# A transformer's first layer: the order of owed work, fillers, taps and divisors

## The chip, the cores and the metric

The kernel runs on one core of one Trainium2 chip. The metric is the device time of one execution in microseconds (us); a time is the median of several executions. PE is the matmul engine (TensorE; PEld are its weight loads), DVE is VectorE, ACT is ScalarE, POOL is GpSimd, and SP issues the DMAs.

## The reference, cut to what matters

Two gated layers run over x (8 sequences of 224 tokens, 512 wide). Each layer is a cross attention on a context of 750 tokens, and a feed-forward part. The change touches the first layer only: 16 heads of 32, and a feed-forward part with ternary weights and a depthwise convolution of three taps.

```
x = x + tanh(g_xattn[0]) * xattn0(layernorm(x), ctx)      # 16 heads, softmax over 750 keys
x = x + tanh(g_ffn[0])   * ffn0(layernorm(x))
    # ffn0: bit_linear 512 -> 2048, conv over 3 tokens, silu, bit_linear 2048 -> 512
x = x + tanh(g_xattn[1]) * xattn1(layernorm(x), ctx, mask) # 8 heads
x = x + tanh(g_ffn[1])   * ffn1(layernorm(x))              # fp4 weights and activations
```

## The kernel before

The program is written out in full, batch after batch: batches n = 0 to 7 are the first layer's attention (`attention16`), n = 8 to 15 the second layer's (`attention8`), and the second layer's feed-forward part closes the kernel. Every engine runs its instructions in the order in which the program issues them.

**A batch of attention16** has two halves. In the first, 16 slots (4 groups of heads, 2 halves of the queries, 2 halves of the context) form the scores of four heads in two pairs of PSUM banks (`ps_pair`, L485); VectorE takes their negated maxima (L493), and ScalarE the exponentials for the sums (L502). Both `ps_pair` tiles are in use by one slot, so the next slot's scores wait for its exponentials. Then the maxima of both context halves are joined (`val`, L526), split into three bf16 parts (`stat_rows`, L427 and L431), and transposed on PE (L437, copied by ScalarE at L439). In the second half, 12 steps form the scores again, transposed and with the maxima taken off (L449, L458), ScalarE takes the exponentials (L601), and PE multiplies them with the values (`products`, L576). What the sums are divided by is worked out in between, in five pieces of the generator `divisors` (named `more`): `less` on VectorE and its exponential on ScalarE (L539, L540); sums, reciprocal and bf16 parts on VectorE (L543 to L546, L427, L431); their transpose (L437, copied at L439); and two spreads over the partitions (L555, copied at L563). The products of two groups are divided at L584.

**Fillers.** Between these fixed parts the program puts pieces of other work, each from a generator that yields its declared cost on PE and on VectorE:

- `values` (L374, copied by ScalarE at L383): 24 pieces of 0.86; `project_out` of the batch before (L398, L409): 8 of 0.86; `ffn0_out` of the batch two before (L1021, L1031): 8 of 0.86.
- `keys_queries` of the next batch: keys (L312, copied by ScalarE at L321) in pieces of 0.63, and between them the norm of x (L172 to L182, `qxn` here), its transposes (L194, copied at L195) and the queries (L341, L350).
- `ffn0` of the batch before, mostly VectorE's: norm and quantization of x (L172 to L177, L182, L880, L859 to L865, L883, L885; one half of x is called fxq here), transposes (L194), spread scales (L210, L213), then eight groups of hidden columns: product (L907, into `ps_t`), scaled by VectorE (L915), the middle tap on ScalarE (L921, `middle`), the outer taps on VectorE (L935), tanh on ScalarE (L965), the gate on VectorE (L947), and a running maximum (L951, L959). Then the second quantization (L986, L989, L1007, L1010).

The tap on ScalarE is not issued at once: `product` puts it on a list (`deferred`), and `put_off` issues what is on it.

**The planner.** `owed` is PE work that was issued ahead of its due, `behind` is VectorE work that was issued and not yet worked off. `fill(us, queues)` takes pieces from the first queue that has any until `owed` reaches us, then takes us off. `pace(us, queues)` takes pieces while `behind` is under us. `finish(queue)` empties a queue and sets `owed` to 0. The queues are `soon` (the first four pieces of values, and project_out), `early` (ffn0_out and the other values), `late` (keys_queries), `beside` (this batch's ffn0) and `old` (what is left of the last one).

```
            self.fill(1.7, soon, early, late)
            if slot == 3:
                self.finish(soon)
                self.finish(old)
            ...
            more = min(max(self.behind - 2.3, 0), 0.5)
            self.fill(1.4 + more, soon, early, late)
            self.behind = max(self.behind - 2.3 - more, 0)
```

**PSUM tiles** on the way of this: `ps_m` (two) for keys, values, projections, queries and their transposes; `ps_t` (one) for the products of ffn0, all spreads and the small transposes; `ps_pair` (two); `ps_pa` (one) for the products with the values.

Of the kernel before, what the change touches and what calls it, by code (L numbers as in the profile page):

```python
# [63 lines left out]
class Net:  # L64
# [122 lines left out]
    def transposed(self, dst, src, i, bank="t"):  # L187

        nc = self.nc
        half = src.dtype == BF16  # L190
        pt = self.ps(bank, [128, KC, TP], BF16 if half else F32)
        ident = self.ident16 if half else self.ident
        for k in range(KC):
            nc.tensor.transpose(pt[:, k, :], src[:, k * 128 : (k + 1) * 128], ident[:TP, :TP])  # L194
        nc.scalar.copy(dst[:, :, i * TP : (i + 1) * TP], pt)  # L195
# [270 lines left out]
    def attention16(self, n, before, ahead, old, soon, early, late, beside):  # L466

        nc, pool, job = self.nc, self.att, self.jobs[n]
        kT, qT = job["kT"], job["qT"]
        rows = [slice(h * 32, (h + 1) * 32) for h in range(4)]


        part = pool.tile([TP, 2, NT, KC, 4], F32, name="part")
        sums = pool.tile([TP, 2, NT, KC, 4], F32, name="sums")
        slots = KC * NT * 2
        self.behind = 1.0  # L480
        for slot in range(slots):
            g, i, c = slot // (2 * NT), slot // 2 % NT, slot % 2
            sc = [self.ps("pair", [TP, 2, 512]) for _ in range(2)]
            for h, r in enumerate(rows):
                nc.tensor.matmul(  # L485
                    sc[h // 2][:, h % 2, :MH],
                    lhsT=qT[r, g, i * TP : (i + 1) * TP],
                    rhs=kT[g][r, c * MH : (c + 1) * MH],
                    start=True,
                    stop=True,  # L490
                )
            for k in range(2):
                nc.vector.tensor_reduce(  # L493
                    part[:, c, i, g, 2 * k : 2 * k + 2], sc[k][:, :, :MH], AX.X, ALU.max, negate=True
                )
            if slot == 0:
                self.finish([before])

                shown = pool.tile([CP, 4, 2 * S], F32, name="p", bufs=2)
            self.put_off()  # L500
            for h in range(4):
                nc.scalar.activation(  # L502
                    shown[:TP, h, :MH],
                    sc[h // 2][:, h % 2, :MH],
                    AF.Exp,
                    bias=part[:, c, i, g, h : h + 1],
                    accum_out=sums[:, c, i, g, h : h + 1],
                )


            self.fill(1.7, soon, early, late)
            if slot == 3:
                self.finish(soon)
                self.finish(old)
            elif slot < 3:
                self.pace(1.0, old)
            if slot in (10, 11):

                self.behind += next(ahead)[1]
            if (slot > 2 or n == 0) and slot < slots - 1:  # L520
                self.pace(1.0, beside)
            more = min(max(self.behind - 2.3, 0), 0.5)
            self.fill(1.4 + more, soon, early, late)
            self.behind = max(self.behind - 2.3 - more, 0)
        val = pool.tile([TP, NT, KC, 4], F32, name="val")
        nc.vector.tensor_tensor(val, part[:, 0], part[:, 1], ALU.min)  # L526
        transposed = self.stat_rows(self.stat[0][n % 2], val.rearrange("p t g h -> p t h g"))
        self.pace(1.0, beside)
        self.fill(1.3, early, late)
        self.finish(early)  # L530
        sT = transposed()
        self.fill(0.7, late)
        self.behind = max(self.behind - 2.5, 0)

        def divisors():

            less = pool.tile([TP, 2, NT, KC, 4], F32, name="less")
            for c in range(2):
                nc.vector.tensor_tensor(less[:, c], val, part[:, c], ALU.subtract)  # L539
            nc.scalar.activation(less, less, AF.Exp)  # L540
            self.behind += 0.4
            yield
            nc.vector.tensor_tensor(sums, sums, less, ALU.mult)  # L543
            total = pool.tile([TP, NT, KC, 4], F32, name="total0")
            nc.vector.tensor_tensor(total, sums[:, 0], sums[:, 1], ALU.add)
            nc.vector.reciprocal(total, total)  # L546
            transposed = self.stat_rows(self.stat_inv, total.rearrange("p t g h -> p t h g"))
            self.behind += 2.2
            yield
            iT = transposed()  # L550
            yield
            for pair in range(2):
                pi = self.ps("t", [128, 2, S])
                for k in range(2):
                    nc.tensor.matmul(  # L555
                        pi[:, k, :],
                        lhsT=self.spread_q[:, 2 * pair + k, :],
                        rhs=iT,
                        start=True,
                        stop=True,  # L560
                    )
                across[pair] = pool.tile([128, 2, S], F32, name="inv")
                nc.scalar.copy(across[pair], pi)  # L563
                yield

        aT = job["aT"] = pool.tile([128, KC, S], F32, name="aT")
        more, across, banks = divisors(), {}, {}

        def products(g, j0, p):

            if g % 2 == 0 and j0 == 0:
                banks["pa"] = self.ps("pa", [128, 2, S])
            for j in (j0, j0 + 1):
                for h, r in enumerate(rows):
                    col = g * 128 + h * 32
                    nc.tensor.matmul(  # L576
                        banks["pa"][r, g % 2, :],
                        lhsT=job["v"][j][:, col : col + 32],
                        rhs=p[:, h, (j - j0) * S : (j - j0 + 1) * S],
                        start=j == 0,  # L580
                        stop=j == NKT - 1,
                    )
            if g % 2 and j0 + 2 == NKT:
                nc.vector.tensor_tensor(  # L584
                    aT[:, g - 1 : g + 1, :], banks["pa"], across[g // 2], ALU.mult
                )
                self.behind += 0.6

        last = None
        for step in range(KC * NKT // 2):  # L590
            g, j0 = divmod(2 * step, NKT)
            pw = [self.ps("pair", [CP, 2, 512]) for _ in range(2)]
            k = kT[g][:, j0 * CP : (j0 + 2) * CP]
            self.weights_minus_max(
                [(pw[h // 2][:, h % 2, : 2 * S], r, g, qT[:, g, :], k) for h, r in enumerate(rows)],
                self.pick, sT, True,
            )
            p = pool.tile([CP, 4, 2 * S], F32, name="p", bufs=2)
            self.put_off()
            for k in range(2):  # L600
                nc.scalar.activation(p[:, 2 * k : 2 * k + 2, :], pw[k][:, :, : 2 * S], AF.Exp)  # L601
            self.behind = max(self.behind - 3.2, 0)
            if last:
                products(*last)
            last = g, j0, p
            if step in (0, 1, 3, 4, 8):
                next(more)
            self.fill(0.5, late)

            self.pace(1.0 if step in (5, 6) else 2.5, beside)  # L610
            self.fill(0.7, late)
        self.finish(late)

        def rest():
            products(*last)
            yield 0.8, 0.6

        return rest()
# [938 lines left out]
```

## Time and profile before

| | us |
|---|---|
| median of 3 runs (2151.72 to 2155.82) | 2153.29 |
| the profiled execution | 2156.02 |
| its span, first to last instruction | 2154.2 |
| PE busy in the span | 2107.8 |
| VectorE busy | 1362.9 |
| ScalarE busy | 1002.1 |
| mean granted PE clock | 0.998 |

The span begins with the first instruction of the program. A row of a timeline has the start, the time from first to last of the merged instructions, engine, line, operation, what is written and read, the count, and in brackets the engine's idle time before it with what ended it. One fp32 matmul stands as two MATMUL rows. A row of windows has the stretch, its length, the busy time and count of PE, PEld, DVE, ACT and POOL, the granted PE clock, the DMA share and GB/s. A row of waits has who waited for whom, the sum in us, the number of times, and the longest.

### The profile page before, as it was taken

The page shows a single profiled execution, that of the slowest core. Times are in us where ns is not written, and L with a number is a line of the kernel's source. Part 1 is how long each engine was busy: PE and PEld are TensorE (multiplying, and loading weights), DVE is VectorE, ACT ScalarE, POOL GpSimd, SP SyncE. Part 2 cuts the span into 40 slices and gives each one's busy share as a digit, 9 for nine tenths or more (in the row PEclk, how much of TensorE's full clock was granted, in tenths as well). Part 3 has the DMA queues.
Part 4 walks back from the last instruction along what each step waited for, and adds up shares of the span by engine and source line. Part 5 has one row for each costly group of instructions (what it writes and reads, how often), then busy time and mean ns, then how long its engine had stood idle before and what let it go on. Part 6 is the DMA issues. An engine that isn't in the chain of part 4 may idle for free.

```text
span 2154.2 us, 32130 instructions
## 1 busy us (share of the span) xinstructions
PE 2107.8 (98%) x12606; PEld 1213.0 (56%) x12606; DVE 1362.9 (63%) x2795; ACT 1002.1 (47%) x2332; POOL 130.3 (6%) x146
## 2 busy tenths in 40 slices
PE   9999999999999999999999999999999999999999
PEld 5444545455554545455656575666656565665555
DVE  3776666677767676674456575654723467776665
ACT  3566667575767667573444343443534331111111
POOL 0000000000000000000000010111100001111111
PEclk9999999999999999999999999999999999999999
DMA  7200010100001010111011112112110011000000
GB/s 226 78 31 29 2 46 2 32 15 18 29 2 46 2 46 21 52 35 52 15 32 52 52 44 66 42 56 69 57 46 11 14 52 41 10 20 20 20 6 20
DMA packets 50215, 81.24 MB, mean 38 GB/s; under 512 B 3344, under 2 KB 29712, under 8 KB 49936
## 3 DMA queue, kind: packets, MB, share of 16 engines
q1 hardware_dynamic: 50064, 79.18, 11.7%
q8 instruction: 100, 1.64, 0.3%
q14 instruction: 51, 0.42, 0.1%
HBM read 65.28 MB, written 13.89 MB: 37 GB/s over the span
## 4 chain that ended last, share of the span: by engine, by line
PE 88%; DVE 5%; ACT 4%; issue 1%; DMA 0%; SPq 0%; POOL 0%; ACTq 0%; POOLq 0%; DVEq 0%
PE ps_m L374 15%; PE ps_m L312 13%; PE ps_big L1168 11%; PE ps_m L1200 6%; PE ps_pair L485 6%; PE ps_m L398 5%; PE ps_m L341 4%; PE ps_half L703 4%; PE ps_half L763 4%; PE ps_pa L666 4%; PE ps_pair L458 2%; ACT p L601 2%; PE ps_pa L576 2%; PE ps_t L907 2%; PE ps_m L1168 2%; PE ps_t L1021 1%
## 5 line engine op out<-in xcount | busy, mean ns | idle before, releaser
L502 ACT ACTIVATE p<-ps_pair,part 112x375 f32<-112x375 f32 x512 | 286.3, 571 | 192.0 <-DVE part L493 192.0
L312 PE MATMUL ps_m<-cx,wk 128*128 128x375 f32 x1024 | 370.5, 491 | 1.3 <-ACT kT L321 1.1
L374 PE MATMUL ps_m<-wv,cx 128*125 128x512 f32 x768 | 355.4, 602 | 0.0
L493 DVE TENSOR_REDUCE part<-ps_pair 112x2 f32<-112x750 f32 x256 | 228.2, 932 | 130.4 <-PE ps_pair L485 128.5
L312 PEld LDWEIGHTS ps_m<-cx,wk 128*128 128x128 f32 x1024 | 179.7, 191 | 118.0 <-issue 34.4
L374 PEld LDWEIGHTS ps_m<-wv,cx 128*125 128x125 f32 x768 | 135.5, 187 | 159.7 <-issue 158.0
L720 DVE CUSTOM_DVE_ANT_0 ps_half<-ps_half,mbias 112x750 f32<-112x750 f32 x128 | 121.1, 946 | 150.7 <-PE ps_half L703 150.0
L601 ACT ACTIVATE p<-ps_pair 125x896 f32<-125x896 f32 x192 | 165.0, 911 | 76.9 <-PE ps_pair L458 76.9
L485 PE MATMUL ps_pair<-kT,qT 32*112 32x375 f32 x1024 | 148.0, 522 | 0.2
L741 ACT ACTIVATE p<-ps_half,nm 112x750 f32<-112x750 f32 x128 | 113.4, 890 | 66.0 <-DVE nm L732 65.6
L1200 PE MATMUL ps_m<-wd,hqT 128*128 128x512 f32 x308 | 136.6, 592 | 0.0
L383 ACT COPY v<-ps_m 125x512 f32<-125x512 f32 x96 | 56.5, 589 | 152.2 <-PE ps_m L374 151.5
L935 DVE SCALAR_TENSOR_TENSOR y<-hp,cw,y 128x224 f32<-128x224 f32 x256 | 109.4, 448 | 20.2 <-ACT y L921 15.7
L398 PE MATMUL ps_m<-wo,aT 128*112 128x512 f32 x256 | 119.6, 602 | 0.0
L1179 ACT ACTIVATE gth<-ps_big 128x352 f32<-128x352 f32 x48 | 22.2, 463 | 206.9 <-PE ps_big L1168 206.9
L341 PE MATMUL ps_m<-xnT,wq 128*128 128x224 f32 x512 | 113.2, 360 | 0.6 <-ACT xnT L195 0.6
L1168 PE MATMUL ps_big<-wu,xqT 128*128 128x352 f32 x352 | 111.3, 459 | 0.0
L1168 PE MATMUL ps_big<-wg,xqT 128*128 128x352 f32 x352 | 111.3, 459 | 0.0
L768 ACT COPY p<-ps_half 125x672 f32<-125x672 f32 x128 | 85.9, 722 | 49.9 <-PE ps_half L763 49.7
L485 PEld LDWEIGHTS ps_pair<-kT,qT 32*112 32x112 f32 x1024 | 52.1, 170 | 98.7 <-ACT p L502 69.6
L502 ACT ACTIVATION_READ_ACCUMULATOR p<-ps_pair,part 112x1 f32 x512 | 103.5, 202 | 0.0
L763 PEld LDWEIGHTS ps_half<-ident,p 112*125 112x125 f32 x768 | 93.2, 189 | 16.1 <-issue 7.8
(223 smaller groups left out, 3026.4 us busy)
## 6 DMA issues: line engine op xcount, KB each, us to landing
cx<-in_ctx SPq DMA_DIRECT2D x32, 750.0 KB, 4.4
wst<-in_w SPq DMA_DIRECT2D x16, 512.0 KB, 8.1
x<-in_x SPq DMA_DIRECT2D x8, 448.0 KB, 6.0
mid<-x SPq DMA_DIRECT2D x8, 448.0 KB, 3.1
x<-mid SPq DMA_DIRECT2D x8, 448.0 KB, 3.5
last<-x SPq DMA_DIRECT2D x8, 448.0 KB, 3.1
out<-yout SPq DMA_DIRECT2D x14, 256.0 KB, 2.0
wraw<-in_w_gate SPq DMA_DIRECT2D x11, 256.0 KB, 2.6
```

What stands on the lines that cost most here:

```text
L312: nc.tensor.matmul(pk, lhsT=self.w["wk"][:, k, g * 128 : (g + 1) * 128], rhs=job["cx"][c][:, k, :], start=k == 0, stop=k == KC - 1,)
L341: nc.tensor.matmul(pq[:, g - g0, :], lhsT=self.w["wq"][:, k, g * 128 : (g + 1) * 128], rhs=xnT[:, k, :], start=k == 0, stop=k == KC - 1,)
L374: nc.tensor.matmul(pv, lhsT=job["cx"][c][:, k, at : at + CP], rhs=self.w["wv"][:, k, :], start=k == 0, stop=k == KC - 1,)
L398: nc.tensor.matmul(po, lhsT=aT[:, g, i * TP : (i + 1) * TP], rhs=self.w["wo"][:, g, :], start=g == 0, stop=g == KC - 1,)
L485: nc.tensor.matmul(sc[h // 2][:, h % 2, :MH], lhsT=qT[r, g, i * TP : (i + 1) * TP], rhs=kT[g][r, c * MH : (c + 1) * MH], start=True, stop= ...
L493: nc.vector.tensor_reduce(part[:, c, i, g, 2 * k : 2 * k + 2], sc[k][:, :, :MH], AX.X, ALU.max, negate=True)
L502: nc.scalar.activation(shown[:TP, h, :MH], sc[h // 2][:, h % 2, :MH], AF.Exp, bias=part[:, c, i, g, h : h + 1], accum_out=sums[:, c, i, g, ...
L601: nc.scalar.activation(p[:, 2 * k : 2 * k + 2, :], pw[k][:, :, : 2 * S], AF.Exp)
L720: nc.vector.tensor_tensor_reduce(out=src, in0=src, in1=masks[i], scale=1.0, scalar=-MASKED, op0=ALU.add, op1=ALU.max, accum_out=mx,)
L763: nc.tensor.transpose(pt[:, j // half, j % half * TP : (j % half + 1) * TP], p[:, h, j * CP : (j + 1) * CP], self.ident[:TP, :TP],)
L1168: nc.tensor.matmul(ps[:, :CW], lhsT=xqT[:, k, :], rhs=wt[:, k, c0 : c0 + CW], start=k == 0, stop=k == KC - 1,)
L1200: nc.tensor.matmul(po, lhsT=hqT[:, k, :], rhs=wd[:, k, :], start=k == 0, stop=k == NC1 - 1)
```

## The change

In the slots: at slot 3, what is left of `soon` and `old` is issued ahead of the filler of 1.7 and not behind it. The second filler of each slot is 1.5 and not 1.4. At the join of the maxima, 1.7 is booked to `behind`, and the pace there goes to 2.7 and not to 1.0. In the steps: ScalarE's put-off taps go ahead of the exponentials only while `behind` is under 4.5, and behind them otherwise. The piece of `divisors` that belongs to a step is issued at the step's end and not ahead of its fillers. Steps 5 and 6 pace to 1.5 and not to 1.0, and a step's last filler is 0.6 and not 0.7. No instruction is added or left out.

```diff
-            self.fill(1.7, soon, early, late)
             if slot == 3:
                 self.finish(soon)
                 self.finish(old)
-            elif slot < 3:
+            self.fill(1.7, soon, early, late)
+            if slot < 3:
                 self.pace(1.0, old)
...
             more = min(max(self.behind - 2.3, 0), 0.5)
-            self.fill(1.4 + more, soon, early, late)
+            self.fill(1.5 + more, soon, early, late)
             self.behind = max(self.behind - 2.3 - more, 0)
...
-        self.pace(1.0, beside)
+        self.behind += 1.7
+        self.pace(2.7, beside)
         self.fill(1.3, early, late)
...
-            self.put_off()
+            late_vector = self.behind > 4.5
+            if self.behind < 4.5:
+
+                self.put_off()
             for k in range(2):
                 nc.scalar.activation(p[:, 2 * k : 2 * k + 2, :], pw[k][:, :, : 2 * S], AF.Exp)
+            self.put_off()
             self.behind = max(self.behind - 3.2, 0)
             if last:
                 products(*last)
             last = g, j0, p
+            self.fill(0.5, late)
+
+            self.pace(1.5 if step in (5, 6) else 2.5, beside)
+            self.fill(0.6, late)
             if step in (0, 1, 3, 4, 8):
+
                 next(more)
-            self.fill(0.5, late)
-
-            self.pace(1.0 if step in (5, 6) else 2.5, beside)
-            self.fill(0.7, late)
         self.finish(late)
```

## What the change will do to the time

> **What bounds the kernel now.** I read the page first, then PE's row of one batch of the first layer, then PE's waits, then single slots in the timeline. Page and windows:
>
> ```profile
> PE 2107.8 (98%) x12606; PEld 1213.0 (56%) x12606; DVE 1362.9 (63%) x2795; ACT 1002.1 (47%) x2332; POOL 130.3 (6%) x146
> ```
>
> ```profile
> 510.80:631.30 120.50, 117.60 (x858) 62.12 (x850) 83.95 (x163) 80.03 (x204) 1.38 (x2) 1.00 0.07 22
> ```
>
> PE sets the end; a batch (n=2 to 6) takes 120.5 us, 2.9 us of it idle by PE's row. The row hides most of the loss. Two consecutive slots of the timeline:
>
> ```profile
> 514.73 0.90 PE L485 MATMUL ps_pair<-kT,qT 32*112 32x375 f32 x8
> ...
> 515.56 2.83 PE L398 MATMUL ps_m<-wo,aT 128*112 128x512 f32 x6
> 515.67 1.79 DVE L493 TENSOR_REDUCE part<-ps_pair 112x2 f32<-112x750 f32 x2
> ...
> 516.70 0.57 ACT L502 ACTIVATE p<-ps_pair,part 112x375 f32<-112x375 f32 x1 [2.12 <-DVE part L493]
> ...
> 518.32 1.64 PE L485 MATMUL ps_pair<-kT,qT 32*112 32x375 f32 x8
> ...
> 519.08 0.27 PEld L485 LDWEIGHTS ps_pair<-kT,qT 32*112 32x112 f32 x4 [0.48 <-ACT p L502]
> ```
>
> Scores unhindered hold PE 0.83 (514.73 to 515.56). Their banks are free again when the fourth exponential is done: 519.08, 4.35 us after the slot began. Here PE had three filler matmuls (2.76 us) and stood in the second half of the next scores: 1.64 instead of 0.90, with no idle time in PE's row. So a slot costs nothing extra if its filler lasts 4.35 - 0.83 = 3.52 us (four pieces of 0.86 and a change of line, 3.6), one piece less costs 0.75, and every us that VectorE comes late to the maxima is added to 4.35. Counted so (start to start, against the shortest of its kind), a batch loses about 8.5 us, not 2.9. The Trainium skill (Trainium Kernel Development and Optimization, Best Practices) says the same of the row: matmul busy time is no measure of the distance to the roofline. By the row a batch could gain 2.9 at most; by start times it can gain or lose more, and I count those.
>
> The waits that are long enough to show as idle:
>
> ```profile
> PE ps_m L194 <- ACT kT L321: 7.5, 8, 2.3
> PE ps_pair L449 <- ACT p L601: 7.2, 21, 0.4
> PE ps_t L907 <- ACT inv L563: 7.2, 6, 1.2
> PE ps_t L907 <- ACT sT L439: 4.7, 9, 1.1
> ```
>
> **How I count.** The planner adds declared costs, so the order after the edit follows by carrying owed and behind through fill and pace; for before this gives exactly the order of PE's rows. Then I walk the queues: every engine in its order, every piece at its duration above or in its own row, a bank free when its reader ends. For before this gives 120.6 us a batch against 120.5, stall by stall near the trace; for after it is an estimate from the same rows.
>
> **1.4 to 1.5, and slot 3's finish ahead of its filler.** Slot 2 gets its fourth piece (the last of project_out), so slot 3 owes nothing and the swap by itself moves at most one piece. Stalls of before, slots 1 to 11: 0.78 + 0.76 + 0.25 + 0.78 = 2.6 (trace 0.74, 0.78, 0.29, 0.76). After: slots 3, 5 and 11 are whole, or nearly. But fxq0 (L182 0.54, L880 0.69, small ones 0.6, L883 0.49, L885 0.43: 2.75) moves from slot 5 to 4 and stands before L1031 (0.75): VectorE has 1.78 + 3.5 in a slot of 4.5, the maxima of slot 5 come 0.8 late, slot 6 stalls 0.7. With 0.05, 0.20 and 0.29 later: 1.25. **-1.3 a batch.** The loads of the next context and x are issued a piece earlier or so in SP's queue; they are used several slots later and land in 4.4 us: nothing. POOL's rstd follows its VectorE step as before, and POOL is idle.
>
> **What the longer filler does at slots 12 to 15.** The keys now run two pieces ahead. In slot 12 the order becomes transposes of xn (ps_m), key group 1's end, L907, then the first piece of key group 2: a third ps_m tile, of which there are two. Both others are emptied by ScalarE copies queued behind this slot's exponentials. They end at 4.35 plus 0.5 of VectorE's lateness, the copy takes 0.53; PE is there at 3.3. Stall 2.2. The nearest row is the same case in batch 0, at its full size:
>
> ```profile
> 80.40 2.16 PE L312 MATMUL ps_m<-cx,wk 128*128 128x375 f32 x6
> ...
> 84.28 0.48 ACT L321 COPY kT<-ps_m 128x375 f32<-128x375 f32 x1
> ...
> 84.81 0.60 PE L194 MATMUL ps_m<-ident,xn 112*128 112x112 f32 x4 [2.25 <-ACT kT L321]
> ```
>
> Behind it on PE stand slot 13's scores; in that pause VectorE and ScalarE catch up, so slots 13 and 14 lose their 0.2 + 0.5. Slot 15 stalls 1.5 (five key pieces in slot 14 last 3.35, and L182 came a slot earlier), against 0.7; the wait of L194 in the val stage (0.7) goes, as key 10's copy is now ahead of the exponentials. Before 2.1, after 3.8. **+1.7.** Bounds of the slot 12 stall: 1.2 (VectorE on time, the shorter copy first) and 2.8 (the largest of its kind, the 2.25 of idle with its lead); 2.2 is nearest the row.
>
> **Divisors at a step's end.** Gained: L907 no longer waits for the copies of sT and inv queued behind exponentials (0.5 and 1.4 walked; the rows' 1.1 and 1.2), and step 3's 0.9 go. In their place the transposes and the spread wait for VectorE to read the product just issued (L915, 0.62): 0.7 and 0.7. But the first piece, less, moves too. Before:
>
> ```profile
> 700.81 0.28 DVE L539 TENSOR_TENSOR less<-val,part 112x32 f32<-112x32 f32 x2
> ...
> 705.07 0.62 DVE L915 TENSOR_TENSOR hp<-ps_t,bc 128x448 f32<-128x448 f32 x1 [3.98 <-PE ps_t L907]
> ...
> 705.81 0.26 ACT L540 ACTIVATE less<-less 112x64 f32<-112x64 f32 x1
> ...
> 707.36 1.72 ACT L601 ACTIVATE p<-ps_pair 125x896 f32<-125x896 f32 x2
> ```
>
> VectorE made less in idle time. After, it comes behind L915, four taps (1.78), L947 (0.62): 705.07 + 0.62 + 1.78 + 0.62 + 0.3 = 708.4, and L540 waits there in ScalarE's queue with middle4 (1.04) and step 1's exponentials behind it: they start near 709.8, not 707.36. Step 2's scores wait for them: 2.2. Bounds: 0 if VectorE kept its lead, 2.4 the whole shift; I see no cover. Steps in all: before 4.2 (1.0 + 0.1 + 1.4 + 1.4 + 0.3), after 5.2 (1.0 + 2.2 + 0.7 + 0.7 + 0.5). **+1.0.**
>
> **The rest.** The taps go behind exponentials only where behind is over 4.5: step 2 alone (5.4), where it frees the banks 1.04 earlier; that is in the 5.2. The booking of 1.7 in the val stage brings the same piece (L951); the 1.5 of steps 5 and 6 and the 0.6 move single query pieces: within 0.2 either way. Fewer changes of line on PE: -0.2.
>
> A batch n=3 to 7: -1.3 + 1.7 + 1.0 - 0.2 = +1.2, walked through 1.1. Batch 2, where owed starts otherwise, +1.8; batch 1 +0.5; batch 0 +1.5. Sum 5 x 1.1 + 3.8 = **+9**.
>
> **The clock.** Where a rule and a row disagree:
>
> ```profile
> 82.60:86.02 3.42, 1.21 (x7) 0.96 (x8) 2.82 (x5) 2.69 (x10) 0.00 (x0) 1.00 0.04 5
> 86.02:89.43 3.41, 3.41 (x12) 1.06 (x11) 0.63 (x1) 0.00 (x0) 0.00 (x0) 0.50 0.37 149
> ...
> 208.89:212.31 3.42, 1.68 (x14) 0.69 (x13) 0.06 (x1) 2.52 (x8) 0.00 (x0) 1.00 0.00 0
> 212.31:215.72 3.41, 3.41 (x10) 1.97 (x7) 3.32 (x3) 2.29 (x9) 0.00 (x0) 0.50 0.00 0
> ```
>
> (PE's busy time is the third number, the granted clock the third from the end.) The Trainium skill (TensorE: Matmul & The Clock Gate, HAM oscillation) asks for no PE gap above about 3.4 us; by it stalls of 2.2 cost nothing more. Here a gap of 2.25 and one of 1.74 inside such a stretch were each followed by 3.4 us at half clock; ten L312 matmuls then took 5.03 from start to start instead of 3.35. I take the row. New stalls of 2.2: slot 12 in five batches, step 2 in seven. With stretches that lie anyhow, one holds 1.74 of it in (3.41 - 2.2 + 2 x 0.46) / 3.41 = 0.62 of the cases: 7 more half-clock stretches, at 1.7 each less what PE would have waited later anyway (slot 15, steps 3 and 4), so about 1.1: **+8**.
>
> **Sum.** 2154.2 of span + 17 = 2171; with the 1.8 around it 2173 against the profiled 2156.0. That execution lies 2.7 above the median, so on the median 2153.3 + 17 = **2170**.
>
> **The rivals.** *Same mechanisms, the clock holds* (0.18): +9, 2162; for it speaks the page's rule, against it both stretches. *More throttling* (0.10): two stretches at most of the twelve stalls, full price: 9 + 18 = +27, 2180. *Cancelled* (0.12): the two new waits are half as long, and no gap is enough: +9 - 6 x 2 = -3, 2150. *Faster* (0.10), by one mechanism: the wait at L540. If VectorE reaches less before ScalarE is through step 0's exponentials and tanh (704.20 + 1.73 + 0.6 = 706.5 or earlier, not 708.4), step 2 loses nothing, and steps gain 1.2 instead of losing 1.0: 7 x -2.2 = -15, so -6 and no clock loss at that place: 2147. It decides at 706.5. Against it speaks 3.0 us of VectorE work that cannot start before L907 ends. That the edit does not do what it says holds in part: the new order of taps and exponentials applies at one step in twelve.
>
> **Numbers.** Likeliest (0.50) 2170, own range 2164 to 2177. Bounds of the two waits, 12 times 1 us, and of the clock, 0 to 18, give 2155 to 2182, which leaves out the faster case and half of the cancelled one. A measurement tells about 0.2% (4.3 us) from no change: slower 0.78, same 0.12, faster 0.10.
>
> **What would show it.** Right: L493's stalls at slots 3, 5, 11 gone; L312 waiting some 2 us for ScalarE in slot 12; L540 waiting for L539 by 2 us, and L449 behind it; more slices of half clock. A first layer shorter than 120.5 a batch, or L449 waiting less than before, would prove me wrong.

## The result and the profile after

The changed kernel takes 2172.45 us (median of 4 runs, 2170.94 to 2173.52) against 2153.72 (4 runs): ratio 1.0086, 95% interval 1.0069 to 1.0104. That is 18.7 us slower; the forecast was 2170. The profiled execution took 2170.94, with a span of 2169.2 against 2154.2; it lies 1.5 below its median, and the one of before (2156.02) 2.3 above, so 15.0 us of the 18.7 can be seen in the two traces.

PE's share in the page, then one batch of the first layer (n=4) in a row of windows, from its first slot to that of the next batch:

```profile
PE 2102.9 (97%) x12606; PEld 1213.3 (56%) x12606; DVE 1364.5 (63%) x2795; ACT 1003.7 (46%) x2332; POOL 130.4 (6%) x146
```

```profile
508.55:630.48 121.93, 116.35 (x851) 61.94 (x850) 84.15 (x164) 80.15 (x204) 1.38 (x2) 1.00 0.07 21
```

The batch lasts 121.93 instead of 120.5, with the same work: PE is idle for 5.6 us of it by its row, before for 2.9. PE's waits show what came and what went:

```profile
PE ps_pair L449 <- ACT p L605: 18.1, 36, 2.2
PE ps_m L312 <- ACT xnT L195: 13.6, 7, 2.0
PE ps_t L437 <- DVE hp L921: 5.0, 7, 0.7
PE ps_t L556 <- DVE hp L921: 4.3, 6, 0.7
PE ps_m L194 <- ACT kT L321: 3.1, 2, 2.2
...
PE ps_t L913 <- ACT sT L439: 0.9, 2, 0.4
```

(The lines of the file moved by up to 6: L907 is L913 now, L539 and L540 are L540 and L541, L601 is L605.) L312's wait for the copy of xn is new, L449's wait for the exponentials grew from 7.2 to 18.1. The product's waits for the copies of sT and inv (4.7 and 7.2) are nearly gone; transposes and spreads wait instead for VectorE to read the product just issued (L921, which was L915).

Slot 12 in the timeline, PE, ScalarE and VectorE:

```profile
563.68 0.90 PE L485 MATMUL ps_pair<-kT,qT 32*112 32x375 f32 x8
...
566.23 0.93 PE L913 MATMUL ps_t<-xqT,w 128*128 128x224 bf16 x8
...
566.40 0.57 ACT L502 ACTIVATE p<-ps_pair,part 112x375 f32<-112x375 f32 x1 [1.56 <-DVE part L493]
...
568.61 0.54 ACT L195 COPY xnT<-ps_m 128x448 f32<-128x448 f32 x1
...
569.21 1.53 PE L312 MATMUL ps_m<-cx,wk 128*128 128x375 f32 x4 [2.05 <-ACT xnT L195]
```

The product ends at 567.2, the next key group needs a third ps_m tile, and the copy that frees one stands behind the slot's four exponentials until 568.61. Slot 12 lasts 6.99 (4.10 before). Steps 0 to 2:

```profile
590.34 1.78 DVE L941 SCALAR_TENSOR_TENSOR y<-hp,cw,y 128x224 f32<-128x224 f32 x4
...
592.57 0.29 DVE L540 TENSOR_TENSOR less<-val,part 112x32 f32<-112x32 f32 x2
...
592.89 0.26 ACT L541 ACTIVATE less<-less 112x64 f32<-112x64 f32 x1 [1.77 <-DVE less L540]
...
593.06 1.02 ACT L927 ACTIVATE y<-hp,cb,cw 128x224 f32<-128x224 f32 x2
...
593.99 1.70 ACT L605 ACTIVATE p<-ps_pair 125x896 f32<-125x896 f32 x2
...
594.93 0.40 PE L449 MATMUL ps_pair<-sT,pick 32*125 32x448 bf16 x2 [0.83 <-ACT p L605]
...
595.73 0.40 PE L449 MATMUL ps_pair<-sT,pick 32*125 32x448 bf16 x2 [0.40 <-ACT p L605]
```

ScalarE stands idle for 1.77 until VectorE has made less behind the taps and the gate; the tap and step 1's exponentials stand behind it, and step 2's scores wait for those.

The stretches at half clock, in rows of windows that lie on the clock's own stretches: slot 12 of batch 4, which got none, then of batch 5; then the wait for less in batches 1 and 4:

```profile
565.07:568.48 3.41, 2.09 (x13) 1.23 (x11) 3.34 (x6) 2.08 (x7) 0.00 (x0) 1.00 0.00 0
568.48:571.90 3.42, 2.69 (x13) 1.26 (x14) 1.92 (x5) 2.44 (x7) 0.00 (x0) 1.00 0.00 0
687.99:691.40 3.41, 1.36 (x11) 0.93 (x9) 3.30 (x7) 3.06 (x11) 0.00 (x0) 1.00 0.00 0
691.40:694.82 3.42, 3.42 (x12) 1.17 (x11) 0.67 (x2) 1.46 (x4) 0.00 (x0) 0.50 0.00 0
...
227.19:230.60 3.41, 1.69 (x18) 0.73 (x18) 3.37 (x7) 1.57 (x4) 0.00 (x0) 1.00 0.00 0
230.60:234.02 3.42, 2.55 (x37) 1.53 (x37) 2.22 (x11) 2.23 (x4) 0.00 (x0) 1.00 0.00 0
592.42:595.83 3.41, 2.18 (x24) 1.42 (x18) 2.10 (x7) 2.94 (x6) 0.00 (x0) 1.00 0.00 0
595.83:599.24 3.41, 3.41 (x50) 2.37 (x53) 3.13 (x14) 2.69 (x5) 0.00 (x0) 1.00 0.00 0
```

It is the same stall of 2.05 us in slot 12 of both batches. In batch 4 it is cut in two by the border of a stretch (PE busy 2.09 and 2.69); in batch 5 it lies inside one (1.36), and the next runs at half clock. That costs 1.65: batch 5 takes 123.58, its neighbours 121.93 and 121.91. Of the five stalls in slot 12 of batches 3 to 7 two were followed by half clock (batches 5 and 7); of the seven waits for less none was.

In the whole trace there are five such stretches, before two: two more in the first layer, and one in the second at 1056 us. The profiled sum: the first slot begins 1.5 earlier (at 29.1 against 30.6; in the traces of the experiments below it begins at 29.2 to 32.8), the first layer's batches take 14.1 more, of which 3.3 is the clock, and what comes behind them 2.4 more: some 1.6 for that one stretch, and 0.5 for a wait of L398 for aT (L585) that is not there before. -1.5 + 14.1 + 2.4 = 15.0.

### The profile page after: what moved, and what is told of

The parts are those of the page before. It is cut to its first block, busy times and chain, and to the rows that moved or that the text cites. A ratio compares the mean times of both kernels' runs of the same rounds, so it can differ in the third digit from the quotient of the medians.

```text
span 2169.2 us, 32136 instructions
## 1 busy us (share of the span) xinstructions
PE 2102.9 (97%) x12606; PEld 1213.3 (56%) x12606; DVE 1364.5 (63%) x2795; ACT 1003.7 (46%) x2332; POOL 130.4 (6%) x146
## 4 chain that ended last, share of the span: by engine, by line
PE 90%; DVE 5%; ACT 4%; issue 1%; DMA 0%; SPq 0%; POOL 0%; ACTq 0%; DVEq 0%
PE ps_m L374 16%; PE ps_m L312 13%; PE ps_big L1174 10%; PE ps_m L1206 6%; PE ps_m L398 5%; PE ps_pair L485 5%; PE ps_m L341 5%; PE ps_half L709 4%; PE ps_half L769 4%; PE ps_pa L672 4%; PE ps_pa L577 3%; PE ps_pair L458 3%; PE ps_t L913 2%; PE ps_m L1174 2%; ACT p L605 2%; ACT p L502 2%
## 5 line engine op out<-in xcount | busy, mean ns | idle before, releaser
L312 PE MATMUL ps_m<-cx,wk 128*128 128x375 f32 x1024 | 369.5, 492 | 14.1 <-ACT xnT L195 13.6
L312 PEld LDWEIGHTS ps_m<-cx,wk 128*128 128x128 f32 x1024 | 181.7, 191 | 129.4 <-issue 29.3
L726 DVE CUSTOM_DVE_ANT_0 ps_half<-ps_half,mbias 112x750 f32<-112x750 f32 x128 | 121.1, 946 | 152.2 <-PE ps_half L709 152.1
L605 ACT ACTIVATE p<-ps_pair 125x896 f32<-125x896 f32 x192 | 165.1, 912 | 67.3 <-PE ps_pair L458 67.3
L485 PE MATMUL ps_pair<-kT,qT 32*112 32x375 f32 x1024 | 137.4, 528 | 3.4 <-ACT p L502 2.8
L398 PE MATMUL ps_m<-wo,aT 128*112 128x512 f32 x256 | 118.0, 600 | 0.5 <-DVE aT L585 0.5
L341 PEld LDWEIGHTS ps_m<-xnT,wq 128*128 128x128 f32 x512 | 91.1, 189 | 22.0 <-issue 18.6
```

Source lines behind the costliest of these rows:

```text
L312: nc.tensor.matmul(pk, lhsT=self.w["wk"][:, k, g * 128 : (g + 1) * 128], rhs=job["cx"][c][:, k, :], start=k == 0, stop=k == KC - 1,)
L341: nc.tensor.matmul(pq[:, g - g0, :], lhsT=self.w["wq"][:, k, g * 128 : (g + 1) * 128], rhs=xnT[:, k, :], start=k == 0, stop=k == KC - 1,)
L398: nc.tensor.matmul(po, lhsT=aT[:, g, i * TP : (i + 1) * TP], rhs=self.w["wo"][:, g, :], start=g == 0, stop=g == KC - 1,)
L485: nc.tensor.matmul(sc[h // 2][:, h % 2, :MH], lhsT=qT[r, g, i * TP : (i + 1) * TP], rhs=kT[g][r, c * MH : (c + 1) * MH], start=True, stop= ...
L726: nc.vector.tensor_tensor_reduce(out=src, in0=src, in1=masks[i], scale=1.0, scalar=-MASKED, op0=ALU.add, op1=ALU.max, accum_out=mx,)
```

## The experiments

All times are medians; "before" is a run of the kernel before on the same chip. Lengths of batch 4 by part, start to start in PE's rows (slots 0 to 11, slots 12 to the val stage, the steps); the last column says how many half-clock stretches the profiled execution had, without the end of the span; one of double length counts as two:

| kernel | us | before | ratio (95%) | slots 0-11 | 12-val | steps | stretches |
|---|---|---|---|---|---|---|---|
| before | 2153.72 | | | 55.86 | 21.86 | 42.82 | 2 |
| after | 2172.45 | 2153.72 | 1.0086 (1.0069 to 1.0104) | 55.12 | 24.04 | 42.76 | 5 |
| a_pa | 2151.10 | 2154.32 | 0.9985 (0.9976 to 0.9993) | 55.13 | 22.17 | 42.77 | 2 |
| a_less | 2159.92 | 2154.32 | 1.0026 (1.0018 to 1.0035) | 55.13 | 25.65 | 41.28 | 4 |
| a_less_pa | 2138.32 | 2154.32 | 0.9927 (0.9912 to 0.9942) | 55.12 | 22.17 | 41.30 | 1 |
| a_14 | 2166.40 | 2154.32 | 1.0062 (1.0045 to 1.0079) | 55.99 | 21.87 | 43.68 | 1 |
| b_15 | 2168.70 | 2153.59 | 1.0068 (1.0053 to 1.0083) | 55.71 | 25.69 | 41.35 | 7 |
| b_end | 2161.77 | 2153.59 | 1.0036 (1.0024 to 1.0049) | 55.86 | 21.86 | 43.51 | 1 |
| b_late | 2152.50 | 2153.59 | 0.9994 (0.9985 to 1.0002) | 55.85 | 21.86 | 42.42 | 2 |
| b_swap | 2160.47 | 2153.59 | 1.0029 (1.0017 to 1.0041) | 56.19 | 21.86 | 42.83 | 3 |
| b_pa | 2144.31 | 2154.82 | 0.9958 (0.9943 to 0.9974) | 55.86 | 21.06 | 42.82 | 1 |
| b_rest | 2150.64 | 2154.04 | 0.9984 (0.9977 to 0.9991) | 55.87 | 21.87 | 42.41 | 1 |
| best | 2131.66 | 2154.82 | 0.9896 (0.9880 to 0.9913) | 55.64 | 21.06 | 41.30 | 0 |
| best2 | 2128.72 | 2154.82 | 0.9884 (0.9869 to 0.9899) | 54.91 | 21.69 | 40.65 | 0 |

(25.65 and 25.69 hold a half-clock stretch of 1.6.) My theory is the prediction's: two new waits, slot 12's third ps_m tile and less in ScalarE's queue, and half-clock stretches behind them. The rivals: the divisors' move costs as a whole; the longer filler costs as such; the clock alone.

**a_pa**, slot 12's wait taken away from the changed kernel:

```diff
-            self.transposed(xnT, xn, i, "m" if n else "t")
+            self.transposed(xnT, xn, i, ("pa" if n <= B else "m") if n else "t")
```

> The changed kernel with one thing undone: the transposes of xn go into ps_pa and not into ps_m, so in slot 12 the first piece of key group 2 finds a free ps_m tile. The order of the work stays. Theory of the prediction: the wait of L312 for ScalarE in slot 12 (2.0 us, 7 times) is gone, and the two stalls of the transposes in ps_m with it; the time falls by some 13 us to about 2159, and by up to 3 more if fewer stretches at half clock follow: 2156 to 2160. Rival, the loss lies in the divisors: 2170 to 2173. Rival, the longer filler costs as such: 2170 to 2173.

Measured 2151.1. L312's wait is gone from PE's waits, and L449's is untouched:

```profile
PE ps_pair L449 <- ACT p L605: 18.0, 36, 2.2
PE ps_t L437 <- DVE hp L921: 5.0, 7, 0.7
PE ps_t L556 <- DVE hp L921: 4.3, 6, 0.7
```

The direction holds, the size was too small by 5 us. A batch gains 1.9 (24.04 to 22.17), which over seven batches is the 13 that I had; batch 1 gains 3.2 (120.77 to 117.61); and three half-clock stretches go, 5 us where I allowed 3. Batches 2 to 7 have none left, though ScalarE still waits 1.77 for less in each: in them half clock follows slot 12's wait, and not that for less.

**a_less**, the other wait taken away:

```diff
             last = g, j0, p
+            if step == 0:
+                next(more)
             self.fill(0.5, late)
...
-            if step in (0, 1, 3, 4, 8):
+            if step in (1, 3, 4, 8):
                 next(more)
```

> The changed kernel with only the first piece of the divisors (less and its exponential) back ahead of the fillers of step 0; the other four stay at the step's end. Theory of the prediction: the exponential of less no longer holds ScalarE's queue, step 2 loses its wait; steps of a batch fall by about 1.5 us, the time by 11 to 16 to 2157 to 2161. Rival, the divisors' move costs as a whole (transposes and spreads that wait for L921): under 3 us gained, 2169 or more. Rival, the clock alone: the wait goes and nearly nothing is gained unless the number of half-clock stretches falls.

Measured 2159.9; the steps fall by 1.48, as expected. The waits are the mirror image of those of a_pa:

```profile
PE ps_m L312 <- ACT xnT L195: 13.6, 7, 2.1
PE ps_pair L449 <- ACT p L605: 8.5, 23, 0.4
```

Transposes and spreads still wait for the read of the product (L923 in this file: 5.7 and 4.3), and the gain of 12.5 is there all the same: the rival that takes the divisors' move as a whole falls. So does the clock alone: this kernel has four stretches, and one fewer than the changed one is worth 1.7.

**a_less_pa**, both edits.

> Both of these at once: the changed kernel with the transposes of xn in ps_pa and the first piece of the divisors ahead of step 0's fillers. Theory of the prediction: both new waits are gone, what the change gains in the slots and in steps 3 and 4 is left: about 15 us under the kernel before, 2136 to 2141, and no stretch at half clock, or one. If the change's gains were not real, or were eaten by something else: 2150 to 2156.

Measured 2138.3, as expected. The gains add up: 21.4 and 12.5 singly, 34.1 together. So the two waits, with the half clock behind them, carry the loss. But not all of the 16 us under the kernel before is the change's own: putting the transposes into ps_pa gains 10.5 on the kernel before too (b_pa below). Measured from there, the change without its two waits gains some 5.5 (1.2 a batch: 119.75 to 118.59).

**a_14**, the changed kernel with the filler back:

```diff
-            self.fill(1.5 + more, soon, early, late)
+            self.fill(1.4 + more, soon, early, late)
```

> The changed kernel with the second filler of a slot back at 1.4. Theory of the prediction: the slots are about as before (slot 12 without its wait, slots 3 to 11 with some of theirs), but step 2's wait for the exponential of less stays, and slot 3's new order shifts pieces: 2162 to 2170. Rival, the longer filler is the whole loss: 2152 to 2156.

Measured 2166.4: the longer filler is not the whole loss. Without it slot 12 has no wait (21.87), ScalarE waits for less as it did (1.77 in batches 2 to 7), and the steps take 43.68. Over half of this trace's loss is in batch 1 (126.65 against 121.02), where the transposes of xn wait 2.87 and 2.16 for a ps_m tile, as in b_swap.

**b_15**, the longer filler alone, on the kernel before (1.4 to 1.5, as above in the other direction).

> The kernel before with one edit: the second filler of a slot is 1.5 and not 1.4. Theory of the prediction: slots 3, 5 and 11 are filled, slot 12 gets the third ps_m tile and its wait of 2 us, L312 for ScalarE in batches 3 to 7, and half-clock stretches after some of them: +4 by the waits alone, +11 with the clock: 2158 to 2165. Rival, the divisors carry the whole loss: 2148 to 2153.

Measured 2168.7, slower than I expected. The waits cost what they should (without a stretch a batch would take 122.74 - 1.65 = 121.1, against 120.5), but each of batches 3 to 7 has a half-clock stretch, and the mean clock falls:

```profile
core 0: 2167.9 us, clock 0.994
```

The stretches of the trace's clock records begin 122.88 us apart, five times running; a batch takes 122.74, so slot 12's stall lies at nearly the same place of a stretch each time.

**b_end**, the divisors at the step's end alone:

```diff
-            if step in (0, 1, 3, 4, 8):
-                next(more)
             self.fill(0.5, late)
...
             self.fill(0.7, late)
+            if step in (0, 1, 3, 4, 8):
+                next(more)
```

> The kernel before with one edit: all five pieces of the divisors at their step's end. Theory of the prediction: step 2 waits 2 us for the exponential of less, steps 3 and 4 lose their waits: +4 by the waits alone, up to +12 with half-clock stretches: 2158 to 2166. Rival, the pieces at the step's end are a gain and the filler is the loss: 2146 to 2150.

Measured 2161.8, inside; the steps take 0.69 more. **b_rest** leaves less where it was and moves the other four only (the same diff, with `step in (1, 3, 4, 8)` at the end and `if step == 0: next(more)` ahead of the fillers).

> The kernel before with pieces two to five of the divisors at their step's end, and less left where it was. Theory: what the move gains in steps 3 and 4 without what less costs, 0.9 a batch: -7, 2147, against +8 measured with less moved too. Rival, the new waits of the transposes and spreads for L915 (0.7 each) take all of the gain: 2152 to 2156.

Measured 2150.6, between the two: 0.41 a batch, half of what I had. So of the move, less costs 1.1 (43.51 - 42.41), and the rest gains 0.4.

**b_late**, the new order of taps and exponentials alone:

```diff
-            self.put_off()
+            if self.behind < 4.5:
+                self.put_off()
             for k in range(2):
                 nc.scalar.activation(p[:, 2 * k : 2 * k + 2, :], pw[k][:, :, : 2 * S], AF.Exp)
+            self.put_off()
```

> The kernel before with one edit: ScalarE's put-off taps go behind the exponentials where behind is over 4.5, which is at step 2 of each batch alone. Theory: step 3's scores lose their wait, 0.8 us a batch: -5, 2149. Rival, the taps only come late and VectorE's taps wait for them: 2153 to 2158.

Inconclusive in time: the interval holds 1. In the trace the steps are 0.40 shorter, half of what I expected.

**b_swap**, slot 3's order alone:

```diff
-            self.fill(1.7, soon, early, late)
             if slot == 3:
                 self.finish(soon)
                 self.finish(old)
-            elif slot < 3:
+            self.fill(1.7, soon, early, late)
+            if slot < 3:
```

> The kernel before with one edit: at slot 3 the owed work goes ahead of the filler of 1.7. The prediction put it at nothing by itself. Walked alone, with the second filler still at 1.4, the owed 0.16 is forgotten and one more piece of 0.86 goes into slot 3, while slots further on run short: +0.4 a batch and more in the first batches, +5: 2159. By the prediction's words: 2152 to 2156.

Measured 2160.5, +6.9: alone it is not nothing. In the trace 6.9 us are in batch 1 (127.89 against 121.02), which has all three half-clock stretches of this run, two of them in a row. They follow waits of the transposes of xn for a ps_m tile, 2.88 and 3.00 in this batch, again slot 12's kind of wait:

```profile
PE ps_m L194 <- ACT kT L321: 9.4, 8, 3.0
```

In the changed kernel, with the filler at 1.5, the swap does nothing that can be seen: slots 1 to 11 take 49.56 in b_15 and 49.55 in the changed kernel. That slots 0 to 11 are 0.59 shorter there than in b_15 is slot 0 alone (6.15 and 5.57), and b_15's last step is shorter by as much (2.24 and 2.82): the same work on the other side of the border.

**b_pa**, the diff of a_pa on the kernel before.

> The kernel before with one edit: the transposes of xn go into ps_pa. The kernel before has the same wait for a third ps_m tile, 2.25 us once in batch 0, once or twice in batch 1, and 0.6 in the val stage of the others, and both its half-clock stretches follow the long ones. Theory: the waits go, -9, and the two stretches with them, -11 in all: 2142 to 2146, granted clock 1.0 all through. Rival, these waits only hide others: 2150 to 2154.

Measured 2144.3, as expected. The two stretches behind the long waits are gone from batches 0 and 1. A stretch of half clock was left in the second layer, where I had expected none.

**best** and **best2**, what the runs pointed to, on the kernel before: the diffs of a_pa and of b_late with 3.5 for 4.5, and

```diff
-            if step in (0, 1, 3, 4, 8):
+            if step in (0, 1):
                 next(more)
...
-            self.fill(0.7, late)
+            self.fill(0.6, late)
+            if step in (2, 4, 7):
+                next(more)
```

and in best2 also

```diff
-            self.fill(1.4 + more, soon, early, late)
+            self.fill((1.5 if slot < 11 else 1.4) + more, soon, early, late)
```

> A version built from what the runs showed, on the kernel before with its fillers of 1.4: transposes of xn in ps_pa; less and the sums at their old place in steps 0 and 1, the transpose and the spreads at the end of steps 2, 4 and 7; taps behind the exponentials where behind is 3.5 or more; last filler of a step 0.6. Theory: -24, 2130, no half-clock stretch. Rival, the parts take from one another: 2138 to 2146.

> The same version, with the second filler 1.5 in slots 0 to 10 and 1.4 from slot 11 on. Theory: slots 3, 5 and 11 are filled without a third ps_m tile: -28, 2126. Rival, the keys still run ahead and the wait in the val stage takes it back: 2130 or more.

Measured 2131.7 and 2128.7: 23.2 and 26.1 us under the kernel before, a little less than expected. What each part of these two versions gives was not run singly. PE's waits of best2, where no ps_m line is left among the longest:

```profile
PE ps_pair L449 <- ACT p L602: 7.3, 21, 0.4
PE ps_t L555 <- DVE hp L919: 4.3, 6, 0.7
PE ps_t L194 <- DVE xn L182: 2.3, 2, 1.5
```

## Why the prediction was right, point by point

**Sum.** Forecast +17, measured +18.7. The order of the work gave +9 in the forecast and 10.8 in the profiled execution (batches 0 to 7: 1.9, -0.3, 2.3 and five times 1.4, where the forecast had 1.5, 0.5, 1.8 and 1.1). The clock gave +8 in the forecast. The four timed executions had a granted clock of 0.9955 in the mean; those of the kernel before that ran beside the experiments had 0.9989. From these I estimate four stretches more ((0.9989 - 0.9955) x 2171 / 0.5 / 3.41 = 4.3), some 7 us at 1.65 each; the two traces differ by three. So the size of this term came out right by luck: seven stretches at 1.1 were forecast, and there were about four at 1.65. Nor did they come where they were forecast: step 2 was counted with seven of the twelve stalls, and none of the seven was followed by half clock in the trace. PE's idle time there is no single gap of 2.2 but 0.83 and 0.40 with work between them, and in batch 4 PE was busy for 2.18 of the stretch. Only in batch 1 is the gap 2.19 long.

**By edit**, for batch 4 and without the clock. The longer filler and the swap: forecast -1.3 + 1.7 = +0.4. The longer filler alone is +0.56 (b_15: 55.71 + 24.04 + 41.35 against 120.54), and the swap on top of it is nothing. All other edits: forecast +1.0 - 0.2 = +0.8, and what is left of 121.92 - 120.54 = 1.38 is +0.82. Of this less is +1.48 (a_less) and the rest -0.66; on the kernel before, the other four pieces alone gain 0.41 (b_rest) and the order of the taps 0.40 (b_late). The forecast had +2.1 for less and -1.3 for the rest: two errors of 0.6 that cancelled.

**Slots 1 to 11.** The forecast counted stalls, from 2.6 to 1.25. Counted in the same way, each row of scores less its unhindered 0.90, batch 4 has 0.74 + 0.78 + 0.29 + 0.73 before (slots 3, 5, 9, 11) and 0.55 + 0.27 + 0.33 after (slots 6, 9, 11): 1.4 less, forecast 1.3. Slots 3 and 5 became whole, slot 11 in part, and slot 6 got a stall because fxq0 came ahead of L1031: right.

```profile
537.18 1.45 PE L485 MATMUL ps_pair<-kT,qT 32*112 32x375 f32 x8
```

In length slots 0 to 11 lost only 0.74, since the longer filler also brings work forward from the steps (42.82 to 41.35 in b_15). So the lengths by part in the table are not to be compared with the forecast's stalls.

**Slot 12.** Forecast 2.2, measured 2.05 of idle time. That the tile is the cause a_pa shows: with a free one the wait is gone.

**Less.** The wait at ScalarE was forecast at about 2 and is 1.77 (12.8 us, 7 times). What it does to step 2 was too large: 2.2 forecast, but with less alone moved back steps 1 and 2 differ by 1.70 (8.77 and 7.07 in a_less). The exponentials of step 1 began 1.9 later in their step than before and not 2.4, and "I see no cover" was wrong. Before, the last of them ended at 709.08 (the last row of the prediction's fence), and PE, busy with other work, came to step 2's scores only at 709.55, so part of the delay was covered:

```profile
709.55 0.41 PE L449 MATMUL ps_pair<-sT,pick 32*125 32x448 bf16 x4
```

**The swap at slot 3.** By itself it was put at nothing. In the changed kernel that is right, because with 1.5 nothing is owed at slot 3; alone it costs 6.9 us (b_swap).

**Sums of the forecast.** Some are off by 0.1: the steps after add up to 5.1, the stalls of slots 12 to 15 to 3.7, and slot 12's terms to 2.1, nearer to the measured 2.05. The outer bounds, 2155 to 2182, do not follow from the terms named for them: twelve times 1 us either way on the +9 and 0 to 18 for the clock give 2150 to 2192.

What stays open: the booking at the join of the maxima, the pace of steps 5 and 6 and the filler of 0.6 were not run singly. Why batches 1 and 2 differ from the others is known in part only (the waits of the transposes in batch 1 of a_14 and b_swap). The one stretch in the second layer follows a wait of PE for VectorE (L194 for xq, 1.9, once) that the kernel before has too. After the change it lies inside one stretch (PE busy 1.52), before it does not (2.30 at the least); but in b_rest it does (1.53), and no half clock followed.

## What to carry to other kernels

A piece that only one engine has to work on for 0.3 us is not cheap if the next engine in line runs in order: ask what stands behind its consumer, and issue it where its producer is idle. When fillers are lengthened, count the PSUM tiles that one slot opens and where the copies that free them stand in their engine's queue. A stall of 2 us can cost 3.7: look whether the granted clock drops behind it.

## What the runs showed of the hardware

In these traces a stretch of half clock is 3.41 us long, or twice that (6.83, in a_pa and b_swap), and in one execution their beginnings differ by whole multiples of that (86.02 and 212.31 before: 37 of them). Whether a stall is followed by one depends on where it lies on this grid. Slot 12's stall of 2.05 us occurs in batches 3 to 7 of three kernels (the changed one, a_less and b_15): ten times it lay inside one stretch, which left PE 1.36 us of work, and half clock followed all ten; five times a border cut it (1.78 to 2.16 us of work in the emptier part), and it followed none. A loop whose length is near a multiple of the grid (b_15: 122.74 against 36 x 3.41 = 122.9) keeps its place on it, and there met half clock in five batches running.

PE's busy time in a stretch does not decide it alone. In the 14 traces each of the 17 stretches with 0.41 to 1.48 us of it was followed by half clock (the end of the span and stretches that are at half clock themselves left out). Of those with 1.50 to 1.89 us ten were and fifteen were not (in the changed kernel 1.89 in batch 0 was, 1.69 in batch 1 was not), and of all those with more, one (2.45, a_less). What decides between these is not shown.
